# Where the channel gate's exponential stands on VectorE, in a two-layer network of a spectral convolution and an involution

## The chip, the cores and the metric

The kernel runs on one NeuronCore of one Trainium2 chip. The metric is the device time of one execution in microseconds (us). TensorE is called PE, VectorE DVE, ScalarE ACT, GpSimd POOL; SP is the engine whose queue issues most of the loads. Everything is float32.

## The reference

The input `x` is 16 images of 16 channels of 256 x 256. Each of two layers normalises `x` by groups of two channels and adds the layer's result to `x`.

Layer 0 is a Fourier-domain operator with learned poles and residues. The change does not touch it. Layer 1 is this:

```python
f = mish(conv2d(xs, W1, b1))                      # each channel alone, 1 -> 4 features, 3x3
top, bot = f[:, :, :H2], f[:, :, H2:]             # upper and lower half of the image
ker = conv2d(relu(conv2d(bot, Wred, bred)), Wspan, bspan)
top_inv = (patches(top) * ker[:, None]).sum(axis=2)          # involution
shuffled = concatenate([ti, roll(bo, -1, axis=1)], axis=3)   # back to 64 planes, 256 x 256
out = mish(conv2d(shuffled, W2, b2))              # 64 -> 16 channels, 3x3
pooled = out.mean(axis=(2, 3))                    # one number per image and channel
gate = sigmoid(Weca[0] * left + Weca[1] * pooled + Weca[2] * right)   # over neighbouring channels
return x * gate[:, :, None, None]
```

All that the second convolution gives to the result is one number per image and channel, the gate. The output of the network is the layer's input plus the normalised input times the gate, so it is written as normalised value times `scale` plus mean.

## The kernel before

Layer 0 fills the first half of the time and leaves the normalised input of layer 1 in DRAM as `zn`, with the groups' means and deviations in `mr`. Layer 1 (`layer1`) then runs over the images.

**Units.** An image is cut into nine units. Unit `n` holds two tiles of 14 useful rows from each half of the image. `Unit.__init__` loads its part of `zn` (tile `z`, eight DMAs on SP's queue). `convolve` (called twice per unit) makes the first convolution: 96 matmuls into banks `c`, and ACT's Mish out of them into `bot` and `wide` (the feature rows). `reduce` makes the involution's reduced map: 16 matmuls into banks `pr`, Relu on ACT into `r`, and it stores `bot` to the DRAM buffer `cf` (POOL's queue). `involution` (called twice) makes 96 matmuls each into four banks `pd`; on DVE the first call gives `t` (L1209), the second `top` (L1211), which is stored to `cf` by eight DMAs on POOL's queue.

**Second convolution.** It runs one image behind. `conv2_rows` loads a 2.2 MB block of rows back from `cf` (SP's queue). DVE forms four `planes` of sums and differences from it, two instructions each (L1263). `conv2` makes four products of 16 matmuls each from them (`c2ps`, L1272) and puts them together on DVE as `even` and `odd` (L1301 to L1305), and ACT applies Mish and adds the values up into `acc` (L1286). An image has eight such blocks. For the last image another form, `conv2_last`, is used, with one DVE instruction (L1313) in place of the planes.

**Gate.** When an image's eight blocks are done, `gate` turns `acc` into 16 numbers: a sum on DVE, one small matmul `pg` (L1345), a multiplication on DVE, `exponential` on DVE (a polynomial, 15 instructions on 128 x 16 values, L860 to L874), then 1/(1+e) and `scale` (L1350 to L1353). Then eight parts of `zn`, loaded two at a time (tile `o`, L1337), are scaled by POOL (L1361) and written to the output (L1370). `gate` is a generator: each `yield` hands control back, and the main loop advances it with `next(last)`.

**Order.** The main loop has one iteration per unit, nine per image: `i = 9 b + s`. The instructions of PE, ACT, DVE and POOL are issued in the order that the program gives (`tc.manual_schedule`); each engine works through its list in that order. SP's DMAs are placed by the framework's scheduler. An iteration does, in this order: the loads for a unit two ahead; `conv2_rows`; `next(last)`; for `s == 8` the start of a new gate; the convolutions of the next unit; the involution of this one; `conv2` of the image before (`s` from 0 to 7), within which the planes of the following block are formed; `reduce` of the next unit; `next(last)` again. At `s == 8`, where an image ends, there is no `conv2`; there DVE forms all four planes of the next image's first block in one go.

**PSUM.** All of layer 1 shares eight banks that are taken in turn. `t` and `top` free the banks of `pd`; the first product of `conv2` takes the bank that the first `t` frees.

Of the kernel before, what the change touches and what calls it, by code (L numbers as in the profile page):

```python
# [856 lines left out]
def exponential(nc, pool, y, tag="exp_b"):  # L857

    n = pool.tile(list(y.shape), F32, tag="exp_n", name="exp_n")
    nc.vector.tensor_scalar(y, y, -88.0, 88.8, ALU.max, ALU.min)  # L860
    nc.vector.tensor_scalar(n, y, float(1 / np.log(2)), ROUND, ALU.mult, ALU.add)
    nc.vector.tensor_scalar(n, n, ROUND, None, ALU.subtract)
    c1 = 0.693359375
    c2 = float(np.float32(np.log(2) - c1))
    nc.vector.scalar_tensor_tensor(y, n, -c1, y, ALU.mult, ALU.add)
    nc.vector.scalar_tensor_tensor(y, n, -c2, y, ALU.mult, ALU.add)

    nc.vector.tensor_scalar(n, n, 127.0, float(1 << 23), ALU.add, ALU.mult)
    bits = pool.tile(list(y.shape), I32, tag=tag, name="exp_b")
    nc.vector.tensor_copy(bits, n)  # L870
    nc.vector.tensor_scalar(n, y, 1 / 5040, None, ALU.mult)
    for c in (1 / 720, 1 / 120, 1 / 24, 1 / 6, 1 / 2, 1.0):
        nc.vector.scalar_tensor_tensor(n, n, c, y, ALU.add, ALU.mult)
    nc.vector.scalar_tensor_tensor(y, n, 1.0, bits.bitcast(F32), ALU.add, ALU.mult)  # L874
# [149 lines left out]
def layer1(ctx, tc, d, zn, cf, mr, nb):  # L1024
# [17 lines left out]
    def bank(shape, name):  # L1042
        return banks.tile([P, *shape], F32, tag="bank", name=name)
# [203 lines left out]
    def conv2_rows(b, s):  # L1247
        t = rows2[(8 * b + s) % 2]
        flat = cf[b % 4].rearrange("(t y) f c x -> (y f c) t x", y=2)
        nc.sync.dma_start(out=t[:, :, 1 : N + 1], in_=flat[:, 16 * s : 16 * s + 17])  # L1250

    def plane(b, s, k):

        t = rows2[(8 * b + s) % 2]
        before, odd, even, after = (t[:, :, x : x + H] for x in (0, 1, H + 1, H + 2))
        x, y, op_ = (
            (before, odd, ALU.subtract),
            (odd, even, ALU.add),
            (odd, even, ALU.subtract),
            (even, after, ALU.subtract),  # L1260
        )[k]
        for rows in (slice(0, 9), slice(9, 17)):
            nc.vector.tensor_tensor(planes[:, k, rows], x[:, rows], y[:, rows], op_)  # L1263
# [61 lines left out]
    def gate(b, acc):  # L1325


        total = sm.tile([P, 1], F32, tag="total", name="total")
        nc.vector.tensor_reduce(total, acc, AX.X, ALU.add)
        totals = sm.tile([P, P], F32, tag="totals", name="totals")  # L1330
        nc.vector.tensor_scalar(totals, zero, total, None, ALU.add)

        def part(k):
            half, c = k % 2, k // 2 * 4
            o = op.tile([P, 4, N + 2], F32, tag="o", name="o")
            src = zn[b, 1 + P * half : 1 + P * half + P, c : c + 4]
            nc.sync.dma_start(  # L1337
                out=o.rearrange("p c x -> p (c x)"), in_=src.rearrange("y c x -> y (c x)")
            )
            return o  # L1340

        parts = [part(0), part(1)]
        yield
        pg = bank([4, H], "pg")
        nc.tensor.matmul(pg[:, 0, :C], lhsT=totals, rhs=wca, start=True, stop=True)  # L1345
        gate = sm.tile([P, C], F32, tag="gate", name="gate")
        nc.vector.tensor_scalar(gate, pg[:, 0, :C], -1.0 / (N * N), None, ALU.mult)
        exponential(nc, sm, gate)
        yield
        nc.vector.tensor_scalar(gate, gate, 1.0, None, ALU.add)  # L1350
        nc.vector.reciprocal(gate, gate)
        scale = sm.tile([P, C], F32, tag="scale", name="scale")
        nc.vector.tensor_tensor(scale, gate, std2[:, b], ALU.add)  # L1353
        yield
        for k in range(0, 8, 2):
            following = [part(k + 2), part(k + 3)] if k < 6 and b == nb - 1 else None
            c = k // 2 * 4
            for half, o in enumerate(parts):
                for i in range(4):
                    eng = nc.vector if i and b == nb - 1 else nc.gpsimd  # L1360
                    eng.tensor_scalar(  # L1361
                        o[:, i],
                        o[:, i],
                        scale[:, c + i : c + i + 1],
                        mean2[:, b, c + i : c + i + 1],
                        ALU.mult,
                        ALU.add,
                    )
                dst = d["out"][b, c : c + 4, P * half : P * half + P]
                nc.gpsimd.dma_start(out=dst.rearrange("c y x -> y c x"), in_=o[:, :, 1 : N + 1])  # L1370
            yield
            if k < 6 and not following:
                following = [part(k + 2), part(k + 3)]
                yield
            parts = following
# [6 lines left out]
    def begin_unit(i):  # L1382
        if i < len(order):
            b, n = order[i]
            units[i] = Unit(b, i, n)

    E = mybir.EngineType
    with tc.manual_schedule(engines={E.PE, E.Activation, E.DVE, E.Pool}):
        begin_unit(0)
        begin_unit(1)  # L1390
        u = units[0]
        u.convolve(0)
        u.convolve(1)
        u.reduce()
        acc, last = None, iter(())
        for i in range(9 * nb + 12):
            b, s = divmod(i, 9)
            now, nxt = units.pop(i, None), units.get(i + 1)
            begin_unit(i + 2)
            if s >= 7 and b < nb:  # L1400
                conv2_rows(b, s - 7)
            if b == nb and 0 < s < 7:
                conv2_rows(b - 1, s + 1)
            if s < 6 and 0 < b < nb:
                conv2_rows(b - 1, s + 2)
            gated = s == 8 and 0 < b <= nb
            next(last, None)
            if gated:
                last = gate(b - 1, acc)
                next(last)  # L1410
            if nxt:
                nxt.convolve(0)
                nxt.convolve(1)
            if now:
                now.involution(0)
                now.involution(1)
            if gated:
                next(last)
            if s == 8 and b < nb - 1:
                for k in (1, 2, 0, 3):  # L1420
                    plane(b, 0, k)
            if s < 8 and b and b <= nb:
                if s == 0:
                    acc = sm.tile([P, 16], F32, tag="acc", name="acc")
                conv2(b - 1, s, acc)
            if nxt:
                nxt.reduce()
            if gated:
                next(last)
            next(last, None)  # L1430

# [143 lines left out]
@with_exitstack  # L1577
def forward(ctx, tc, d):
    nb = d["x"].shape[0]
    dram = ctx.enter_context(tc.tile_pool(name="dram", bufs=1, space=DRAM))  # L1580
    keep = ctx.enter_context(tc.tile_pool(name="keep", bufs=1))
    al = dram.tile([17, 4, 2, C, nb, 2, N], F32, name="al")
    bd = dram.tile([nb, P, P], F32, name="bd")
    hd = dram.tile([2, 2, 64, 2, nb // 2, C, N], F32, name="hd")
    tabs = (
        dram.tile([P, C // 2, 4, N], F32, name="td"),
        dram.tile([NF, P, 384], F32, name="avd"),
        dram.tile([P, 2, C, N], F32, name="ed"),
    )
    zn = dram.tile([nb, N + 2, C, N + 2], F32, name="zn")  # L1590
    cf = dram.tile([4, N + 2, 4, C, N], F32, name="cf")
    mr = keep.tile([P, nb, G, 2], F32, name="mr")
    layer0_forward(tc, d, al, bd, tabs)
    layer0_mix(tc, d, al, hd, tabs)
    layer0_back(tc, d, hd, bd, zn, mr, tabs[2])
    layer1(tc, d, zn, cf, mr, nb)
# [25 lines left out]
```

## Time and profile before

| | us |
|---|---|
| median of 3 runs | 5901.66 (5900.02 to 5911.2) |
| the profiled execution, its own time | 5909.89 |
| its span in the trace | 5908.1 |
| layer 1, from the start of its steady part to the last image | about 3240 to 5800 |
| mean distance from one image's end to the next in that part | 182.7 |

The mean distance is that between the starts of the eight planes at `s == 8`, from 3239.9 to 5615.5 us, over 13. In the prediction's lines, a row of a timeline gives the start in us, the busy time in us, the engine, the line of the kernel, the operation and the tiles, and in brackets how long the engine stood idle before it and what ended that. A row of waits gives who waited for what, with total us, number of times and longest. In a row of stretches, the numbers are the length and the busy time of PE, weight loads, DVE, ACT and POOL with instruction counts, then the granted PE clock, the share of the DMA engines and GB/s.

### The profile page before, as it was taken

How to read it: one execution, taken by the hardware profiler on the slowest of the kernel's cores; microseconds unless marked ns; L12 is line 12 of the kernel's file. 1: busy time of each engine (PE TensorE's matmuls, PEld its weight loads, DVE VectorE, ACT ScalarE, POOL GpSimd, SP SyncE). 2: the span in 40 equal slices, each digit the busy share in tenths (PEclk: the TensorE clock that was granted, in tenths of full speed). 3: DMA queues.
4: the chain of work that ended last, by engine and by line, in shares of the span. 5: the costliest groups of instructions: out<-in, count | busy, mean ns of one | idle time of the engine just before them, and what ended most of it. 6: DMA issues, size and time to landing. Idle time of an engine off the chain costs nothing.

```text
span 5908.1 us, 216564 instructions
## 1 busy us (share of the span) xinstructions
PE 5447.1 (92%) x94280; PEld 3319.2 (56%) x94280; DVE 4671.7 (79%) x8643; ACT 2324.0 (39%) x4158; POOL 2831.1 (48%) x4090
## 2 busy tenths in 40 slices
PE   6999999698898898999899999999999999999996
PEld 5888988677677676777544333433333333334332
DVE  8888988478888786888658878878877778787784
ACT  2444556344444442222244333433433343334331
POOL 1334444433333335666553555545555455554453
PEclk9999999899999999999899999999999999999998
DMA  3455555555556657999787988889888898888886
GB/s 98 137 148 156 168 141 148 157 194 191 194 201 197 202 193 268 326 327 327 246 236 224 284 280 265 260 253 281 279 268 250 252 289 270 277 255 254 272 278 233
DMA packets 814470, 1370.07 MB, mean 232 GB/s; under 512 B 139824, under 2 KB 629168, under 8 KB 798384
## 3 DMA queue, kind: packets, MB, share of 16 engines
q1 hardware_dynamic: 596176, 881.61, 47.3%
q0 software_dynamic: 217344, 474.61, 25.9%
q8 instruction: 740, 12.12, 0.9%
q14 instruction: 210, 1.72, 0.1%
HBM read 729.78 MB, written 556.47 MB: 218 GB/s over the span
## 4 chain that ended last, share of the span: by engine, by line
PE 55%; DVE 10%; issue 2%; DMA 1%; ACT 1%; POOL 0%; SPq 0%; DVEq 0%; ACTq 0%; POOLq 0%
PE c2ps L1272 15%; PE pd L1194 15%; PE c L1144 12%; DVE planes L1263 2%; PE pr L1172 2%; PE py L951 2%; PE py L952 2%; PE ph L760 2%; PE ps L706 2%; DVE zb L983 1%; DVE st L968 1%; PE pg L725 1%; PE pf L940 1%; PE pt L741 1%; DVE o L963 1%
## 5 line engine op out<-in xcount | busy, mean ns | idle before, releaser
L1263 DVE TENSOR_TENSOR planes<-rows 128x1152 f32<-128x1152 f32 x960 | 1180.4, 1293 | 7.0 <-PE c2ps L1272 6.9
L1224 POOL DMA_DIRECT2D cf<-top x1152 | 667.8, 691 | 929.3 <-DVE top L1211 775.3
L1194 PE MATMUL pd<-wide,dw 32*32 32x512 f32 x27648 | 988.6, 597 | 28.2 <-issue 28.0
L1144 PE MATMUL c<-z,w 18*64 18x512 f32 x13824 | 801.5, 595 | 16.2 <-DMA z<-zn 15.8
L1194 PEld LDWEIGHTS pd<-wide,dw 32*32 32x32 f32 x27648 | 542.2, 103 | 459.4 <-issue 175.2
L1209 DVE TENSOR_TENSOR t<-pd,r 128x512 f32<-128x512 f32 x576 | 357.7, 683 | 384.9 <-PE pd L1194 384.6
L1144 PEld LDWEIGHTS c<-z,w 18*64 18x64 f32 x13824 | 319.6, 131 | 491.0 <-issue 352.0
L1242 POOL DMA_DIRECT2D cf<-bot x720 | 386.3, 590 | 320.8 <-DMA cf<-top 114.4
L780 POOL TENSOR_TENSOR h<-w 128x256 f32<-128x256 f32 x258 | 211.3, 819 | 576.4 <-DVE w L774 572.4
L1211 DVE TENSOR_TENSOR top<-pd,t 128x512 f32<-128x512 f32 x576 | 357.7, 683 | 131.7 <-PE pd L1194 131.6
L1361 POOL TENSOR_SCALAR o<-o,scale,mean 128x258 f32<-128x258 f32 x488 | 386.1, 799 | 151.6 <-DVE scale L1353 133.6
L1272 PE MATMUL c2ps<-planes,c 128*32 128x512 f32 x3968 | 454.7, 594 | 3.4 <-DVE planes L1313 3.4
L1153 ACT ACTIVATE bot<-c,b 128x512 f32<-128x512 f32 x576 | 365.0, 685 | 171.1 <-issue 137.3
L964 POOL TENSOR_TENSOR x<-x,o 128x512 f32<-128x512 f32 x256 | 324.5, 1267 | 214.5 <-DVE o L963 214.5
L205 PE MATMUL pu<-fy,f 128*128 128x128 f32 x2048 | 414.3, 285 | 0.3 <-ACT u L219 0.3
L1298 ACT COPY mid<-c2ps 128x512 f32<-128x512 f32 x120 | 70.5, 588 | 867.3 <-PE c2ps L1272 867.3
L212 PE MATMUL pv<-at,f 128*128 128x128 f32 x2048 | 402.4, 279 | 0.0
L322 POOL DMA_DIRECT2D al<-o x544 | 338.1, 628 | 117.0 <-ACT o L313 80.9
L1161 ACT ACTIVATE wide<-c,b 128x512 f32<-128x512 f32 x576 | 365.3, 694 | 0.0
L706 PE MATMUL ps<-tt,lt 64*32 64x256 f32 x8448 | 291.8, 386 | 59.2 <-issue 21.1
L725 PE MATMUL pg<-alb,s 128*32 128x64 f32 x16896 | 284.7, 221 | 60.6 <-issue 42.4
L951 PE MATMUL py<-h,iy 128*128 128x256 f32 x1024 | 316.1, 390 | 11.2 <-DMA h<-hd 11.2
(244 smaller groups left out, 10180.0 us busy)
## 6 DMA issues: line engine op xcount, KB each, us to landing
rows<-cf SPq DMA_DIRECT2D x128, 2176.0 KB
cf<-top POOLq DMA_DIRECT2D x896, 112.0 KB, 7.0
cf<-bot POOLq DMA_DIRECT2D x336, 224.0 KB, 6.1
z<-zn SPq DMA_DIRECT2D x576, 129.0 KB
alb<-alx SPq DMA_DIRECT2D x132, 512.0 KB
zn<-zb SPq DMA_DIRECT2D x128, 516.0 KB
o<-zn SPq DMA_DIRECT2D x128, 516.0 KB
z<-in_x SPq DMA_DIRECT2D x64, 1024.0 KB
```

The source lines that it names most:

```text
L205: nc.tensor.matmul(pu[:, h, :, :, e].rearrange("p v g m -> p (v g) m"), lhsT=f[:, e, c, h], rhs=fy[:, e].rearrange("p (n m) -> p n m", m=2 ...
L212: nc.tensor.matmul(pv[:, a, h], lhsT=f[:, e, c, h], rhs=at[:, e, 4 * cg + c].rearrange("p l m -> p (l m)"), start=e == 0, stop=e == 1,)
L706: nc.tensor.matmul(ps[32 * g : 32 * g + 32, odd, v], lhsT=lt[lanes, kk, g, 1 - v : 3 - v].rearrange("p l c -> p (l c)"), rhs=tt[lanes, kk, g],
L951: nc.tensor.matmul(py[:, e], lhsT=iy[:, e], rhs=h[:, e, k % 4], start=True, stop=False)
L1144: nc.tensor.matmul(ps[half, a][to : to + 64], lhsT=w1[lanes, dx], rhs=self.z[lanes, c : c + 2, dx : dx + N], start=dx == 0, stop=dx == 2,)
L1161: nc.scalar.activation(self.feat[:, c : c + 2, 1 : N + 1], ps[0, a], AF.Mish, bias=b1[0])
L1194: nc.tensor.matmul(out[32 * k : 32 * k + 32], lhsT=dw[lanes, kernel, dx], rhs=self.feat[lanes, 2 * k : 2 * k + 2, dx : dx + N], start=dx == 0,
L1224: nc.gpsimd.dma_start(out=rows[y + 2 * lo : y + 2 * hi, :, c + 2 * k : c + 2 * k + 2].rearrange("y f c x -> y f (c x)"), in_=o[32 * k + 2 ...
L1242: nc.gpsimd.dma_start(out=rows[y + 4 * lo : y + 4 * hi, to : to + n].rearrange("p c x -> p (c x)"), in_=src.rearrange("p c q x -> p (c q x)"),
L1263: nc.vector.tensor_tensor(planes[:, k, rows], x[:, rows], y[:, rows], op_)
L1272: nc.tensor.matmul(ps[32 * j : 32 * j + 32], lhsT=w[:, blk], rhs=src[:, 4 * j + blk : 4 * j + blk + 4], start=(i, blk) == (0, 0), stop=(i, ...
L1361: eng.tensor_scalar(o[:, i], o[:, i], scale[:, c + i : c + i + 1], mean2[:, b, c + i : c + i + 1], ALU.mult, ALU.add,)
```

## The change

`gate` gets one more `yield`, ahead of the exponential. The main loop takes the gate's later parts at other places, for all images but the last. At `s == 8` only the parts up to the multiplication behind `pg` are issued. The exponential is issued at the end of the next iteration (`s == 0`), behind that unit's involution and the second convolution. The end of the gate (L1350 to L1353 of before) is issued at the start of the iteration after (`s == 1`), ahead of its convolutions, and the scaling of the first two parts at that iteration's end. The loads, scalings and stores of the other parts follow in the iterations after, two iterations later than before. The last image's own gate keeps its order.

```diff
         nc.vector.tensor_scalar(gate, pg[:, 0, :C], -1.0 / (N * N), None, ALU.mult)
+        yield
         exponential(nc, sm, gate)
         yield
...
             gated = s == 8 and 0 < b <= nb
-            next(last, None)
+            if s or b > nb:
+                next(last, None)
             if gated:
                 last = gate(b - 1, acc)
                 next(last)
...
             if nxt:
                 nxt.reduce()
-            if gated:
+            if gated and b == nb:
                 next(last)
-            next(last, None)
+            if not gated or b == nb:
+                next(last, None)
```

## The prediction

> **What bounds the kernel now.** I read the page first (shares and the chain that ended last), then the waits of TensorE inside layer 1, then the timeline of VectorE and of TensorE around one end of an image, then the granted clock just after it.
>
> ```profile
> span 5908.1 us, 216564 instructions
> ...
> PE 5447.1 (92%) x94280; PEld 3319.2 (56%) x94280; DVE 4671.7 (79%) x8643; ACT 2324.0 (39%) x4158; POOL 2831.1 (48%) x4090
> ...
> PE 55%; DVE 10%; issue 2%; DMA 1%; ACT 1%; POOL 0%; SPq 0%; DVEq 0%; ACTq 0%; POOLq 0%
> ```
>
> TensorE bounds the kernel. A saving must therefore be time in which TensorE stands still or runs slowly. The waits of TensorE from 3240 to 5800 us, where layer 1 runs steadily (total us, times, longest):
>
> ```profile
> PE c2ps L1272 <- DVE t L1209: 39.5, 14, 3.3
> PE pd L1194 <- issue: 26.9, 26, 2.3
> ```
>
> Fourteen waits, one per image, all before the first c2ps product of the step behind an image's end, all for `t`. The timeline of VectorE at one of them (start us, us, line; the exponential's middle instructions left out):
>
> ```profile
> 3962.93 2.48 DVE L1211 TENSOR_TENSOR top<-pd,t 128x512 f32<-128x512 f32 x4 [0.62 <-PE pd L1194]
> 3965.33 0.16 DVE L1347 TENSOR_SCALAR gate<-pg 128x16 f32<-128x16 f32 x1
> 3965.53 0.18 DVE L860 TENSOR_SCALAR gate<-gate 128x16 f32<-128x16 f32 x1
> ...
> 3968.57 0.17 DVE L874 SCALAR_TENSOR_TENSOR gate<-exp_n,exp_b 128x16 f32<-128x16 f32 x1
> 3968.66 9.70 DVE L1263 TENSOR_TENSOR planes<-rows 128x1152 f32<-128x1152 f32 x8
> 3978.28 0.17 DVE L1350 TENSOR_SCALAR gate<-gate 128x16 f32<-128x16 f32 x1
> 3978.48 0.25 DVE L1351 RECIPROCAL gate<-gate 128x16 f32<-128x16 f32 x1
> 3978.84 0.17 DVE L1353 TENSOR_TENSOR scale<-gate,std 128x16 f32<-128x16 f32 x1
> 3978.95 2.48 DVE L1209 TENSOR_TENSOR t<-pd,r 128x512 f32<-128x512 f32 x4
> ```
>
> From 3962.93 to 3981.4 VectorE has no gap: in this step it is VectorE that is late. TensorE at the same place, and at the next image's end:
>
> ```profile
> 3970.16 6.60 PE L1194 MATMUL pd<-wide,dw 32*32 32x512 f32 x192
> 3979.69 1.92 PE L1272 MATMUL c2ps<-planes,w_sum 128*32 128x512 f32 x16 [2.92 <-DVE t L1209]
> ...
> 3987.71 6.13 PE L1144 MATMUL c<-z,w 18*64 18x512 f32 x96
> ...
> 4165.49 3.19 PE L1272 MATMUL c2ps<-planes,w_sum 128*32 128x512 f32 x16 [2.92 <-DVE t L1209]
> ...
> 4175.22 5.41 PE L1144 MATMUL c<-z,w 18*64 18x512 f32 x96
> ```
>
> pd is done at 3976.77; c2ps needs a PSUM bank that the first `t` (end 3979.64) frees. Sixteen products take 1.92 us in one case and 3.19 in the other. The granted clock says why (stretches behind the wait at 3250; the last number but two is the clock):
>
> ```profile
> 3248.00:3250.70 2.70, 0.00 (x0) 0.00 (x0) 2.63 (x7) 0.00 (x0) 0.51 (x1) 1.00 0.25 82
> 3250.70:3252.70 2.00, 1.96 (x12) 0.53 (x16) 2.00 (x4) 0.00 (x0) 1.70 (x5) 0.63 0.92 310
> 3252.70:3254.70 2.00, 2.00 (x16) 0.56 (x12) 2.00 (x4) 0.59 (x1) 1.95 (x4) 0.51 1.09 361
> 3254.70:3257.00 2.30, 2.30 (x28) 0.68 (x24) 2.30 (x3) 0.00 (x0) 2.30 (x2) 1.00 1.04 309
> ```
>
> **The change, part by part.** The change removes and adds no instruction on VectorE. For the 15 gates before the last, the exponential (15 instructions, 3965.53 to 3968.75 = 3.22 us) and the end of the gate (L1350 to L1353, 3978.36 to 3978.95 = 0.59 us) leave the stretch between `top` and the next `t`. They now stand, adjacent, behind the next step's planes and ahead of the `t` after that. Call the steps 8 (image's end), 0, 1, 2.
>
> *Step 8 to step 0.* `t` comes 3.22 + 0.59 = 3.81 us earlier. The 14 waits are 2.11 to 3.27 us, so all of them go: 39.5 us. What is late next is TensorE itself: `t`'s first bank would be free 0.9 us before pd ends. No row is needed earlier than it is there: the first rows of the next image were issued at 3918.29 and 3938.18, over 40 us ahead of their planes.
>
> *Slow restart.* From c2ps's start to pd's start in step 0 there are 14.07 to 14.09 us in 3 cases, 14.77 to 15.06 in ten, 16.25 in one. Without trouble it is 7.00 + 1.02 + 5.35 = 13.4 (c2ps, pr, c). The fast cases lose 0.7 because VectorE is late for ACT's `odd` and `r`, whose banks c waits for (c 6.13 instead of 5.41); after the change VectorE is 0.9 us earlier against TensorE here, which covers that. Summed over the 14: 21 us. The Trainium skill, TensorE: Matmul & The Clock Gate (What's actually happening), has the clock halve only after an idle window of about 3.4 us; by that rule gaps of 2.9 would cost nothing and about 11 x 1.65 = 18 of these 21 us would stay. The trace shows 0.51 to 0.63 right behind a gap of 2.75, so I take the trace: 21.
>
> *Step 0 to step 1, the price.* Count from T, pd's end in step 8. `t` starts at T - 1.63 (3978.95 - 3.81 = 3975.14, against 3976.77). From there to the last plane VectorE has 17.16 us without a gap (3978.95 to 3996.11), then 3.81 of moved work: free at T + 19.4, first `t` of step 1 done at T + 20.05. TensorE ends pd of step 1 at T + 13.4 + 6.73 = T + 20.1. A tie: I take 0.05 us of wait. In the trace `t` then waited 1.13 us for pd; now it is behind pd by over 2 us, so step 1 looks like today's fast step 0 (first `t` ends as c2ps starts), with its 0.7 us in c. Cost 0.75 x 14 = 10.5 us. In step 2 VectorE is free 16.4 us after that c2ps's start and pd's first half is done at 17.5: caught up. Bounds: 0 if ACT happens to be early, 2 us a time if VectorE is slower than counted.
>
> *POOL and SP.* The scaling by POOL (8 instructions, 2 stores a step) goes from the ends of steps 8, 0, 1, 2 to those of 1, 2, 3, 4, and of SP's queue the loads of later parts go with it (behind the rows of steps 2 to 5 instead of 0 to 3). Nothing on TensorE's path waits for POOL's stores; its 133.6 us of waiting for `scale` (16 times) all but go. I cost the move at nothing: the same 1 MB in and 1 MB out a step, later by two steps. The cover is rows loaded well ahead: those issued at 4023.54 are first read at 4049.97, 26 us later, where the slowest landing I see is 16.8 us (5818.67 to 5835.47). Against the change speaks the Trainium skill, SBUF — State Buffer (SBUF: two separate sides): a VectorE operation with two SBUF inputs and a GpSimd operation share a port pair, and whichever comes second is blocked whole. Eight scalings of 0.554 us, each blocking once, would be 4.4 us of VectorE a step, more than step 2's slack of 1.1. The rows say: six planes take 7.30 us alone and 7.51 to 7.59 beside scaling (timeline), so 0.3 us, and the slack holds. POOL pays instead (four scalings up to 7.07 us); in the steps that scale it is busy 14.3 to 17.4 us of 20 to 21. So zero, not 4.4.
>
> *The tail.* At the last image's last step the same exponential holds back L1313: TensorE waits 3.35 us and its 16 products take 3.48 instead of 1.94: 4.9 us won. The exponential then delays step 1's L1313: `odd` ends about 5798.2, plus 3.81 and 2.44 of planes is 5804.5, where TensorE wants it at 5802.6: 2 us lost. Later TensorE waits 6.5 us for rows at 5835.58; SP issues them behind part loads both before and after, by my count at about the same time, so between 1.5 and 7 us of the gain gets through. I take 4, from -6 to +8.
>
> **Sum.** 39.5 + 21 - 10.5 + 4 = 54 us. The profiled execution took 5909.9 us (span 5908.1): 5856. The median of the runs, 5901.66, is 8 us lower: 5848.
>
> **Rivals.** (1) *The wait moves to step 1.* The tie at T + 20.1 is tight. If VectorE comes 2 us later than counted, TensorE stands 2 us before c2ps in step 1 and restarts slowly (+1): of (39.5 + 21 - 10.5) / 14 = 3.57 us an image 0.6 is left, 8 in all plus the tail: about 5890. For it: no slack by my sum. Against: every duration in it was read beside POOL's scaling, which in step 0 is now gone.
> (2) *A row load comes late: slower.* In SP's queue part loads wait for the stores before them (501.9 us in all, longest 10.2) and hold the rows behind. If now in each image one row load for steps 4 to 7 slips more than the 9.6 us by which it is early today (26.4 - 16.8), TensorE stands as in the tail, 6.5 us: 14 x 6.5 = 91 lost against 54 won: 5939. For it: DMA share is 0.83 to 0.93 from 4070 to 4110 without these transfers. Against: steps 1 to 3 carry them now at up to 1.02 and rows are never waited for before the tail.
> (3) *Only the wait goes, the clock stays as it is* (another cause of the slow products): 39.5 - 10.5 + 4 = 33, 5869. It lies in the main forecast's range.
>
> **Chances.** The forecast with its bounds (5828 to 5880, rival 3 included) 0.80; rival 1 (5880 to 5900) 0.10; rival 2 (above 5913) 0.10. This measurement tells 0.2% (11.8 us) from no change: faster means below 5890. Of rival 1 a third lies there: 0.83 faster, 0.07 same, 0.10 slower. The range 5828 to 5888 takes in the forecast and part of rival 1.
>
> **What would show it.** Right: the 14 waits of c2ps for `t` gone or moved to step 1 with a few tenths each; w_sum at 1.92 in nearly all steps; exponential and reciprocal adjacent; image period 182.7 down to about 179; POOL's wait for `scale` only at the end. Wrong: waits of c2ps in step 1 of 2 us; VectorE waiting for rows before 5790; stalls "issue" of pd grown well over 27 us.

## The result, and the profile after

The changed kernel took 5849.15 us (median of 5 runs, 5843.26 to 5856.29) against 5901.66 of before (5 runs, 5894.91 to 5911.23). The ratio is 0.9906, 95% interval 0.9889 to 0.9923. Measured a second time, beside other kernels on one chip, it was 0.9893 (0.9875 to 0.9910). The forecast was 5848.

The page of the changed kernel, the profiled execution of 5856.29 us:

```profile
span 5854.5 us, 216537 instructions
...
PE 5425.1 (93%) x94280; PEld 3313.5 (57%) x94280; DVE 4664.1 (80%) x8643; ACT 2322.4 (40%) x4158; POOL 2863.9 (49%) x4090
...
PE 69%; DVE 17%; DMA 8%; issue 4%; ACT 1%; POOL 1%; SPq 0%; DVEq 0%; ACTq 0%; POOLq 0%
```

The first two lines say what was expected: 22 us less busy TensorE, and as many instructions on VectorE as before. The third must not be set against its counterpart of before. There the shares add up to some 70% of the span, here to nearly 100%: the chain was followed back further, into layer 0. It does not say that VectorE grew on the path.

The waits of TensorE from 3240 to 5740 us:

```profile
PE pd L1194 <- issue: 28.9, 36, 2.3
PE c2ps L1272 <- issue: 3.3, 2, 2.2
```

The line "c2ps <- DVE t" with its 39.5 us is gone, not smaller. VectorE's timeline at an image's end and in the step behind it (middle of the exponential left out):

```profile
3960.09 0.16 DVE L1347 TENSOR_SCALAR gate<-pg 128x16 f32<-128x16 f32 x1
3960.17 9.70 DVE L1263 TENSOR_TENSOR planes<-rows 128x1152 f32<-128x1152 f32 x8
3969.79 2.47 DVE L1209 TENSOR_TENSOR t<-pd,r 128x512 f32<-128x512 f32 x4
...
3987.39 0.17 DVE L860 TENSOR_SCALAR gate<-gate 128x16 f32<-128x16 f32 x1
...
3991.09 0.18 DVE L1354 TENSOR_TENSOR scale<-gate,std 128x16 f32<-128x16 f32 x1
3991.19 2.48 DVE L1209 TENSOR_TENSOR t<-pd,r 128x512 f32<-128x512 f32 x4
```

The planes now follow `gate` directly and `t` follows the planes directly; the 3.8 us of gate work stand ahead of the next step's `t`. TensorE over the same time:

```profile
3965.90 6.60 PE L1194 MATMUL pd<-wide,dw 32*32 32x512 f32 x192
3972.43 1.92 PE L1272 MATMUL c2ps<-planes,w_sum 128*32 128x512 f32 x16
...
3985.79 7.31 PE L1194 MATMUL pd<-wide,dw 32*32 32x512 f32 x192
3993.03 1.92 PE L1272 MATMUL c2ps<-planes,w_sum 128*32 128x512 f32 x16
```

c2ps starts where pd ends (3972.43 against 3965.90 + 6.60), in both steps. And the granted clock there (the last number but two) is full:

```profile
3972.00:3976.00 4.00, 4.00 (x51) 1.18 (x40) 3.80 (x6) 0.59 (x1) 1.96 (x4) 1.00 1.09 363
```

**A finer measure than the time.** The start of each step's first `pr` matmul in TensorE's timeline gives the length of every step. Averaged over 14 images, in us (undisturbed, step 8 takes 13.2, step 0 20.5, the others 19.89):

| kernel | step 8 | step 0 | step 1 | step 2 | steps 1 to 7 together | image |
|---|---|---|---|---|---|---|
| before | 13.41 | 24.85 | 21.51 | 21.04 | 144.56 | 182.82 |
| changed | 13.54 | 20.62 | 20.58 | 20.07 | 144.37 | 178.53 |
| changed, second trace | 13.39 | 20.51 | 20.26 | 19.99 | 144.09 | 177.99 |

The gain is in step 0. Splitting the execution at the first image's end (the first L1329), the 15th and the last: layer 0 and the first image took 3223.0 us before and 3230.1 after, the 14 images 2559.5 and 2499.4, the tail 90.9 and 90.0 (the rest, behind the last image's L1329, is 34.8 and 34.9). The code ahead of the first mark is the same; over all the traces of this study the mark lies between 3217.6 and 3241.5 us. That scatter of 24 us is in every total below. The steps are free of it.

### The profile page after: what moved, and what is told of

The parts are those of the page before. It is cut to its first block, busy times and chain, and to the rows that moved or that the text cites. A ratio compares the mean times of both kernels' runs of the same rounds, so it can differ in the third digit from the quotient of the medians.

```text
span 5854.5 us, 216537 instructions
## 1 busy us (share of the span) xinstructions
PE 5425.1 (93%) x94280; PEld 3313.5 (57%) x94280; DVE 4664.1 (80%) x8643; ACT 2322.4 (40%) x4158; POOL 2863.9 (49%) x4090
## 3 DMA queue, kind: packets, MB, share of 16 engines
q8 instruction: 740, 12.12, 0.9%
## 4 chain that ended last, share of the span: by engine, by line
PE 69%; DVE 17%; DMA 8%; issue 4%; ACT 1%; POOL 1%; SPq 0%; DVEq 0%; ACTq 0%; POOLq 0%
PE pd L1194 17%; PE c2ps L1272 15%; PE c L1144 13%; DMA z<-in_x 5%; PE ph L760 4%; PE ps L706 4%; PE pg L725 3%; PE pr L1172 3%; PE py L951 2%; PE py L952 2%; PE pt L741 2%; DVE st L167 2%; DVE zb L983 1%; DVE st L968 1%; PE px L306 1%
## 5 line engine op out<-in xcount | busy, mean ns | idle before, releaser
L1362 POOL TENSOR_SCALAR o<-o,scale,mean 128x258 f32<-128x258 f32 x488 | 421.0, 871 | 58.5 <-DVE scale L1354 44.9
```

The source lines that it names most:

```text
L1362: eng.tensor_scalar(o[:, i], o[:, i], scale[:, c + i : c + i + 1], mean2[:, b, c + i : c + i + 1], ALU.mult, ALU.add,)
```

## The experiments

The theory: TensorE waited for `t` because VectorE did 3.8 us of gate work ahead of it, and moving that work is the gain. The rivals: the gain comes from the output's work, which moved too; or the work moved costs as much where it went. The changed kernel's second measurement had its expectation too:

> The changed kernel itself, beside the next three on one chip. Both theories: 0.989 to 0.992 of before, as when it was first measured. Step 0 near 20.6 us, step 1 near 20.6, no wait of c2ps for t. If the mean over steps 1 to 7 moves by 1 us or more from the 144.4 us of the first trace, differences of that size between the other kernels' single traces are noise.

Measured: 0.9893, step 0 at 20.51 us, step 1 at 20.26, no wait of c2ps for `t`; steps 1 to 7 moved by 0.28 us. The two traces of experiment 4 differ by 0.65 us there, so between single traces only differences of about 1 us or more can be read.

The kernels were measured in three groups, each on one chip with runs of before beside it (1 to 4; 6 to 8 with the changed kernel's second measurement; 5, 9 and the second half of 4). Every ratio is to those runs of before. The step times are from one trace for each kernel.

**1. Only the output later.** VectorE as before; loads, scalings and stores of the output two steps later.

```diff
             gated = s == 8 and 0 < b <= nb
-            next(last, None)
+            if s > 1 or b > nb:
+                next(last, None)
...
             if gated:
                 next(last)
-            next(last, None)
+            if b > nb or (gated and b == nb) or (s and not gated):
+                next(last, None)
```

> The kernel before, with the exponential and the end of the gate where they were on VectorE, and only the loads, scalings and stores of the output moved two steps later, as in the changed kernel. Theory (VectorE's 3.8 us between top and t is what TensorE waits for): same as before within 10 us; the 14 waits of c2ps for t stay at about 2.8 us, and step 0 at about 24.9 us. Rival (the gain comes from POOL's and the DMAs' output work leaving the end of the image): 40 to 55 us faster than before, step 0 near 20.6 us. In both, TensorE's pauses in steps 1 to 7 should shift from steps 1 to 4 to steps 3 to 6, if they follow the output's traffic.

Measured: 0.9989 (0.9973 to 1.0004), step 0 at 24.76 us. TensorE's waits in layer 1:

```profile
PE c2ps L1272 <- DVE t L1209: 39.6, 14, 3.2
PE pd L1194 <- issue: 25.0, 28, 1.7
```

The waits stay, all 14. The pauses did move with the output: step 2 fell from 21.04 to 19.98 and step 5 rose from 20.29 to 21.32, and steps 1 to 7 together stayed (144.15). So the output's move alone gives nothing that stands clear of the noise, and VectorE's order is what the gain needs.

**2. The exponential left out, everything else as before.**

```diff
-        exponential(nc, sm, gate)
         yield
         nc.vector.tensor_scalar(gate, gate, 1.0, None, ALU.add)
```

> The kernel before without the exponential (15 VectorE instructions for each of the 16 gates are left out, so the gate's values are others); the end of the gate stays between planes and t. Theory: the 3.22 us are enough to end nearly all 14 waits, so step 0 falls to about 20.6 us, and there is no price in step 1: 59 to 65 us faster than before in the body, 3 to 5 more in the tail, and 3.2 at the very end where the last gate is on the path: 60 to 72 us in all, so 10 to 18 us faster than the changed kernel. Rival (the price in step 1 is nothing): within 8 us of the changed kernel beyond the 3.2 us of the last gate.

Measured: 0.9916 (0.9895 to 0.9936), 48.5 us faster than before, where 60 to 72 were expected. Step 0 is 20.46, as expected: 3.22 us less on VectorE are enough. But steps 1 to 7 stand at 145.07. The theory's number missed; the rival's, about as fast as the changed kernel, came nearer. Less work was not faster than work moved away. What differs besides from the changed kernel is the output's place (experiments 4 to 6) and the end of the gate, 0.6 us on VectorE, which stayed ahead of `t`.

**3. The exponential twice in the new place**, for the first 14 gates.

```diff
+        if b < nb - 2:
+            spare = sm.tile([P, C], F32, tag="spare", name="spare")
+            nc.vector.tensor_scalar(spare, gate, 1.0, None, ALU.mult)
+            exponential(nc, sm, spare, tag="spare_b")
         exponential(nc, sm, gate)
```

> The changed kernel with the exponential done twice in its new place for the first 14 gates (16 more VectorE instructions a time, about 3.4 us). Theory (VectorE has no slack left at the start of step 1): c2ps waits for t in step 1 instead, about 3.3 us each, with a slow restart behind it: 4 to 5 us an image, 55 to 70 us slower than the changed kernel, so about as slow as before (0 to 15 us slower). Rival (there is slack behind step 0): at most 20 us slower than the changed kernel.

Measured: 0.9978 (0.9964 to 0.9993). The wait is back, one step later (waits of TensorE, and its timeline at one of them):

```profile
PE c2ps L1272 <- DVE t L1209: 35.1, 13, 3.3
```

```profile
3991.03 6.60 PE L1194 MATMUL pd<-wide,dw 32*32 32x512 f32 x192
4000.56 3.32 PE L1272 MATMUL c2ps<-planes,w_sum 128*32 128x512 f32 x16 [2.94 <-DVE t L1209]
```

Step 1 takes 24.30 us instead of 20.26 to 20.58: 3.7 to 4.0 us. The added work is 3.23 us (3992.79 to 3996.02 on VectorE in one image), and 6 of the 13 waits are 2.92 to 2.94 us: the start of step 1 had only 0.3 us of room beyond the exponential that was moved there. The rest of the 3.7 to 4.0 us is the slow restart, which followed 11 of the 13 waits. In total the kernel is 0.7 to 0.9% slower than the changed one, some 40 to 50 us, a little less than the 55 to 70 of the theory, since step 2 catches up fully (19.95).

**4. Output one step later instead of two, twice measured.** VectorE's order is that of the changed kernel; the first scaling is issued at the end of step 0.

```diff
             if not gated or b == nb:
                 next(last, None)
+            if s == 0 and b <= nb:
+                next(last, None)
+                next(last, None)
```

> The changed kernel, with the exponential, the end of the gate and the first scaling all at the end of step 0: VectorE's order is unchanged from the changed kernel, and the output runs one step later than in the kernel before, not two. Theory: within 8 us of the changed kernel, that is 45 to 60 us faster than before; no wait of c2ps for t. Rival (the output's place matters): half of the gain is lost, 20 to 30 us faster than before.

> The kernel with the output one step later, a second time. Theory (POOL waits for scale with step 1's stores queued behind it, and the pile of transfers stops TensorE in step 2): 0.993 to 0.996 of before again, step 2 near 21 to 22 us with pauses of 2 us and more, steps 1 to 7 at 145 us or more. Rival (the first measurement was chance): 0.989 to 0.991, step 2 near 20.0 us.

Measured: 0.9942 (0.9923 to 0.9962), and again 0.9946 (0.9925 to 0.9966): about 0.5% above the changed kernel's second measurement and 0.4% above its first. The first expectation of the theory (within 8 us) was wrong, and the first measurement was not chance. The step times say where: step 0 20.59 and 20.53, step 1 20.41 and 20.59, but step 2 21.90 and 21.61 against 20.0. POOL's waits in the first of these traces:

```profile
POOL o L1362 <- DVE scale L1354: 73.2, 14, 5.9
```

The changed kernel's POOL has no such wait before the last gate. What it does here, in POOL's timeline (first scaling, its first store, the stores of `top`, the second pair):

```profile
4366.85 2.19 POOL L1362 TENSOR_SCALAR o<-o,scale,mean 128x258 f32<-128x258 f32 x4 [5.47 <-DVE scale L1354]
4369.34 0.84 POOL L1371 DMA_DIRECT2D out_dram<-o  x1 [0.30 <-POOL o L1362]
...
4375.68 4.66 POOL L1224 DMA_DIRECT2D cf<-top  x8
...
4386.77 2.19 POOL L1362 TENSOR_SCALAR o<-o,scale,mean 128x258 f32<-128x258 f32 x4
```

`top` was complete at 4371.5 on VectorE; its eight stores start at 4375.68, behind the scalings. Two pairs of output parts and the stores of two steps then come close together. TensorE's timeline and the stretches (DMA share second from last):

```profile
4390.80 3.89 PE L1194 MATMUL pd<-wide,dw 32*32 32x512 f32 x42 [3.87 <-issue]
```

```profile
4370.00:4380.00 10.00, 10.00 (x139) 3.40 (x139) 10.00 (x12) 4.18 (x10) 9.65 (x14) 1.00 0.75 236
4380.00:4390.00 10.00, 6.93 (x176) 3.21 (x161) 6.30 (x8) 3.46 (x6) 6.43 (x12) 1.00 1.00 309
4390.00:4400.00 10.00, 9.20 (x82) 2.33 (x85) 4.83 (x6) 0.59 (x1) 6.87 (x13) 0.66 1.04 362
```

The DMA share goes from 0.75 to over 1, and TensorE pauses in the middle of pd. That the waiting scaling is what brings the transfers together is read from this one timeline; no run separates it from the place of the output as such. A wait at the head of POOL's queue need not cost anything: in the kernel before, POOL waited for `scale` for 90.8 us in the same stretch, 14 times, and experiment 1, which ends these waits, changed steps 1 to 7 by 0.4 us only.

**5. The exponential left out, and the output two steps later**: the edits of experiments 1 and 2 together.

```diff
-        exponential(nc, sm, gate)
         yield
...
-            next(last, None)
+            if s > 1 or b > nb:
+                next(last, None)
...
-            next(last, None)
+            if b > nb or (gated and b == nb) or (s and not gated):
+                next(last, None)
```

> The kernel before without the exponential (the gate's values are others), with the output's loads, scalings and stores two steps later as in the changed kernel; the end of the gate stays between planes and t. Theory (the kernel without the exponential was no faster than the changed one because its first scaling stands in POOL's queue waiting for scale and holds back the stores of step 0, which then bunch with the output's traffic): steps 1 to 7 fall from 145.1 to about 144.0 us, and the time is 5 to 20 us below the changed kernel's 0.989 to 0.991 of before: 0.986 to 0.989. Rival (the output's place has no part in it; moving the exponential is as good as leaving it out): 0.989 to 0.992 again, steps 1 to 7 at 145.

Measured: 0.9881 (0.9857 to 0.9906), steps 1 to 7 at 143.99 us. Against experiment 2 the steps behave as the theory said (145.07 to 143.99, and the 14 images from 2508.0 to 2492.9 us), by 1.1 us from one trace each. The interval of the total reaches over 0.9906, so the total alone would not decide it. The 14 images take as long as in the changed kernel's second trace (2491.8): with the output in the same place, moving the exponential is worth as much as leaving it out.

**6. The output one step later still.**

```diff
-            if s or b > nb:
+            if s not in (0, 2) or b > nb:
                 next(last, None)
...
-            if not gated or b == nb:
+            if (not gated or b == nb) and (s != 1 or b > nb):
                 next(last, None)
```

> The changed kernel with the output's loads, scalings and stores one step later still (ends of steps 2 to 5), VectorE's order the same. Theory that only VectorE's place counts: within 8 us of the changed kernel. Rival (the pauses of TensorE depend on which steps carry the output: one step later cost about 20 us against two): a further difference of 10 us or more in one direction or the other, with the pauses in steps 4 to 7.

Measured: 0.9886 (0.9869 to 0.9903), beside 0.9893 of the changed kernel; steps 1 to 7 at 144.08 against 144.09. Three steps are no different from two. Steps 3 and 7 change places (21.57 to 19.93, 20.06 to 20.85): the pauses travel, their sum stays.

**7. The exponential in two halves**, on top of experiment 6.

```diff
-        exponential(nc, sm, gate)
-        yield
+        halves = exponential_halves(nc, sm, gate)
+        next(halves)
+        if b < nb - 1:
+            yield
+        next(halves, None)
+        if b == nb - 1:
+            yield
         nc.vector.tensor_scalar(gate, gate, 1.0, None, ALU.add)
...
-            if s not in (0, 2) or b > nb:
+            if s > 2 or b > nb:
                 next(last, None)
...
-            if (not gated or b == nb) and (s != 1 or b > nb):
+            if not gated or b == nb:
                 next(last, None)
```

> As the kernel with the output three steps later, but with the exponential in two halves: 7 instructions (1.5 us) at the end of step 0, the other 8 and the end of the gate (2.3 us) at the end of step 1. Theory (step 1 pays about 0.7 us because VectorE comes late): step 1 falls by 0.5 to 0.7 us, step 2 rises by at most 0.3, in all 3 to 8 us faster than the kernel with the output three steps later. Rival (no price in step 1): the same step times within 0.2 us.

Measured: 0.9883 (0.9862 to 0.9903). The median over the images goes from 19.92 to 19.90 in step 1 and from 20.11 to 19.89 in step 2. There was hardly a price in step 1 to save; 0.2 us of one stood in step 2. The rival came closer.

**8. The output's work left out** for the first 14 images.

```diff
-        parts = [part(0), part(1)]
+        parts = [part(0), part(1)] if b >= nb - 2 else None
...
         nc.vector.tensor_tensor(scale, gate, std2[:, b], ALU.add)
         yield
+        if b < nb - 2:
+            return
```

> The changed kernel with the loads, scalings and stores of the output left out for the first 14 images (their outputs are not written; the gate is still computed). Theory (TensorE's pauses in steps 1 to 7 come from the DMA traffic of the output): steps 1 to 7 fall from about 144.4 to 140 to 141 us (139.2 without any pause, 0.7 for step 1), so 45 to 60 us faster than the changed kernel. Rival (the pauses come from the kernel's other traffic): at most 15 us faster, and steps 1 to 7 stay above 143 us.

Measured: 0.9817 (0.9798 to 0.9837), 49 us below the changed kernel's second measurement; steps 1 to 7 at 140.49 us. TensorE's waits from 3233 to 5675 us shrink to one line:

```profile
PE pd L1194 <- issue: 4.0, 4, 2.9
```

So most of the pauses are there because of the output's transfers, scalings and stores. The pauses counted as waits fell by some 23 us against the changed kernel's second trace (25.5 in pd and 1.4 ahead of c2ps); what else makes up the 50 us of the 14 images was not separated.

**9. The output spread over eight steps**, one part a step, for the first 14 images.

```diff
+        for k in range(8 if b < nb - 2 else 0):
+            o, c = parts.pop(0), k // 2 * 4
...
+            nc.gpsimd.dma_start(out=dst.rearrange("c y x -> y c x"), in_=o[:, :, 1 : N + 1])
+            yield
+            if k < 6:
+                parts.append(part(k + 2))
+                yield
-        for k in range(0, 8, 2):
+        for k in range(0, 8 if b >= nb - 2 else 0, 2):
```

> The changed kernel with the output of the first 14 images spread over eight steps: one part loaded, scaled and stored a step, from step 1 to the next image's end, instead of two parts a step in four steps. Theory (TensorE's pauses grow faster than the DMA traffic of a step): steps 1 to 7 fall from 144.1 to 142 to 143 us, 10 to 30 us faster than the changed kernel, 0.984 to 0.988 of before. Rival (the pauses follow the sum of the traffic, wherever it lies): within 8 us of the changed kernel.

Measured: 0.9916 (0.9896 to 0.9937), not faster than the changed kernel. Steps 1 to 7 are at 144.03, the same sum again, and step 8, which now carries a part too, rose to 14.01. The theory of this run is wrong: halving the traffic of a step did not lower the pauses. The spreading is not even: the last two parts are scaled one behind the other (at 4122.74 and 4126.13 us in one image).

No version here that does the whole work is shown to beat the changed kernel: the intervals of experiments 6 and 7 overlap with its own.

## Why the prediction was right

**The 14 waits and the slow restart** (39.5 and 21 us forecast, 60.5 together). Step 0 fell by 24.85 - 20.62 = 4.23 us, 59.2 us over 14 images. Experiment 1 shows that the output's move is not the cause, experiment 3 that the wait comes back where the work is put. The restart can be counted: from c2ps's start to `pr` the four products take 7.00 us undisturbed; of the 41 waits for `t` in the traces of before and of experiments 1 and 3, 33 were followed by 8.4 us or more. In step 0 they took 8.4 to 9.9 us in 11 of 14 images before, and 7.00 us in all 28 images of the changed kernel's two traces: of the 59.2 us, 39.5 are the waits and 19.4 these products. Taking the trace's clock was right. By the idle window of about 3.4 us that the prediction cites from the Trainium skill (TensorE: Matmul & The Clock Gate, What's actually happening), some 18 us of this would not have come.

**The price in step 1** (10.5 us forecast) is the term that failed. Two readings in it were off.

First, "17.16 us without a gap" was read in a step where POOL scaled beside the first two planes. The same two planes in the kernel before and in the changed one:

```profile
3983.74 2.77 DVE L1263 TENSOR_TENSOR planes<-rows 128x1152 f32<-128x1152 f32 x2
```

```profile
3974.86 2.48 DVE L1263 TENSOR_TENSOR planes<-rows 128x1152 f32<-128x1152 f32 x2
```

VectorE is free at T + 18.9 instead of 19.4 (in one image c2ps starts at 4148.52 in step 0 and `t` at 4167.44). The tie was not quite one: in all 28 images of the two traces the first `t` of step 1 is done at least 0.27 us before c2ps starts. That there is not much more room, experiment 3 shows.

Second, the 0.7 us in the c behind these products hardly came. That c takes 5.33 to 5.56 us in the 28 images, against 5.34 undisturbed: 1.0 us over the 14 images of the first trace and 1.3 us over those of the second, where 10.5 were forecast. In 8 of 14 images of the second trace step 1 takes no more than 19.91 us; what the others lose lies in pd and c2ps, not there.

**POOL and SP at nothing.** The number was right: steps 1 to 7 together went from 144.56 to 144.37 and 144.09. The reason given, that nothing on TensorE's path waits for POOL's stores, was not enough. Experiments 4 and 5 show that the place of the output is worth about 1 us an image. Had the change moved the output by one step, this zero would have been wrong by some 20 us. That two steps cost nothing is therefore partly luck: the prediction had no ground for telling two steps from one.

**The tail** (4 us forecast) gave 0.9 us in the first trace and nothing in the second (91.0 us against 90.9). TensorE there:

```profile
5751.63 1.92 PE L1272 MATMUL c2ps<-planes,c 128*32 128x512 f32 x16 [1.83 <-DVE planes L1313]
...
5778.65 7.06 PE L1272 MATMUL c2ps<-rows,c 128*32 128x512 f32 x48 [6.10 <-DMA rows<-cf]
...
5799.08 5.43 PE L1272 MATMUL c2ps<-rows,c 128*32 128x512 f32 x48 [1.07 <-DMA rows<-cf]
...
5809.10 5.43 PE L1272 MATMUL c2ps<-rows,c 128*32 128x512 f32 x48 [1.15 <-DMA rows<-cf]
```

The 1.83 us of the exponential is the 2 us forecast. The rows that come late cost 8.3 us in three waits, 6.5 us and one of 0.25 before: the start was earlier, the rows were not. No run was made for the tail.

**The sum** came out at 54 us against 53.6 between the two profiled executions, and part of that is luck: the 14 images gained 60.0 us where 50 were forecast (nearly all of it the price that did not come), the tail 3 us less than forecast, and the part ahead of the first mark happened to be 7.1 us slower.

**The rivals.** No wait moved to step 1 (rival 1), no rows came late before the tail (rival 2), and the clock did change, as the 7.00 us in step 0 show (rival 3).

## What to carry to other kernels

Look for the step in which an engine that otherwise has gaps has none, and ask what of its work there nobody needs yet; 3.8 us of small instructions moved into a step with room gave 4.2 us an image. Where the work that depends on it starts matters too: with the output one step later instead of two, its scaling waiting for `scale` with stores behind it, two fifths to a half of the gain was lost, though which of the two costs it was not separated. Where a chip's runs scatter by more than the effect, compare the lengths of the same steps in two traces.

## What the runs showed of the hardware that was not expected

TensorE's clock dropped behind short waits (granted 0.63 and 0.51 behind a wait of 2.75 us in the prediction's lines): of 41 waits between 1.78 and 3.28 us, 33 were followed by about 1.4 to 3 us lost in the next four products (8.4 to 10.0 us instead of 7.0), 8 by nothing, among them waits of 2.11 and 2.93 us. The wait's length did not decide it.

TensorE pauses in the middle of independent matmuls ("issue", up to 4.2 us). The traces show what it waits for: its own instructions. The queue q8 of the page ("instruction") moves 740 packets of 16,384 bytes, 12.12 MB. TensorE has 189,628 instructions in the trace (94,280 matmuls, 94,280 weight loads and some for its sequencer). That makes 64 bytes an instruction and 256 instructions a packet. Counted in this stream, all 405 such pauses in the 13 traces (3240 to 5740 us) stand at the same place, instruction 193 or 194 modulo 256. Each ended 1.0 to 1.9 us after a packet of q8 had landed, 396 of them 1.0 to 1.65 us after; a moment taken at random lies 1.0 to 1.65 us behind such a landing in 9% of cases.

In layer 1 the pauses in pd were 20.6 to 39.6 us in the traces with the output's work and 4.0 us without it. With that work, 93 of 358 and 101 of 359 packets (the changed kernel's two traces) landed less than 1.9 us before their first instruction started; without it 51 of 362. So the output's work makes the instructions come late, and how it does so no run here shows. A high DMA share is not the sign of it: in the 5 us ahead of the changed kernel's pauses of over 0.3 us the median share was 0.86 and 0.89, at random moments 0.95 and 0.96. Which steps pause follows the output's place. The sum of steps 1 to 7 stayed at 144.0 to 144.4 us in six kernels whose output starts two steps later or more (experiment 3, with its added wait, is left aside), and was 145.0 to 145.6 in experiments 2 and 4.
